# Re-ordering the borders of a four-layer graph network kernel: opening, layer changes, last round, and filler work for TensorE

## The chip, the cores and the metric

The kernel runs on one core of a Trainium2 chip. Time is device time in microseconds (us) of one execution. The kernel before takes 2108.0 us (median of 3 runs, 2107.67 to 2110.47). All runs of a timed comparison are compared with runs of the kernel before on the same chip. The changed kernel was not run again beside the experiments, which had other rounds on five chips; the kernel before had medians of 2107.0 to 2107.6 there, and 2108.59 beside the changed kernel. So a timed difference of some 1.5 us or less shows nothing by itself; there I go by the stages of the traces. A profiled execution also gives a trace, whose span is some 1.8 us shorter than its measured time (2103.9 for 2105.65).

## The reference

Four layers, each `x = x + layer(relu(layernorm(x)))`, on x of 128 samples x 64 nodes x 256 features, in float32:

```python
# layer 0: aggregate with the normalized adjacency, two products, two batch norms
A_norm = A + eye(n);  deg = A_norm.sum(0) + A_norm.sum(1) - diag(A_norm)
A_hat = A_norm * dinv[:, None] * dinv[None, :]           # dinv = rsqrt(deg)
agg = einsum('nm,bmd->bnd', A_hat, h)
out = batchnorm(relu(batchnorm(agg @ W1.T + b1)) @ W2.T + b2)
# layer 1: two graph convolutions, then LSTMs over windows of p = 1, 2, 3, 4 nodes
h = relu(einsum('ts,bsh->bth', adj, h @ Wg0 + bg0))
h = relu(einsum('ts,bsh->bth', adj, h @ Wg1 + bg1))
for p in 1..4: h[:, last node of each window] = lstm_last(h's windows of p nodes)
# layer 2: causal attention, one head;  layer 3: attention with 4 heads, masked by adj == 0
```

## The kernel before

The 8192 rows of x go in 16 chunks of 512. Layer 0 takes the first 268 us. Layer 1 goes by eight superchunks of two chunks, in which the LSTM's products fill TensorE and the convolutions of the next chunks are put in as units at chosen places (`CONV`). Layers 2 and 3 run interleaved, one `ROUND` a chunk, with a `FIRST` and a `LAST` round. Within these regions the program's order is the order of the instructions on each engine that is listed. So an instruction that waits can hold back those that stand behind it on its engine: a VectorE copy in the profile after (50.93) stands behind a step that waits 1.54 us.

```python
    with tc.manual_schedule(engines={PE, DVE, Pool, SP}):        # opening (engine names cut)
        xt = load0(0)                        # 512 KB of input
        ...                                  # adjacency, 4 small loads, then the weights
        an, dinv = degrees(setup)            # VectorE
        mv, rstd = ln_stats(xt, "a0")
        normalized(setup, an, dinv)          # scale, transpose on TensorE, scale
        ln_apply(hs[0], xt, mv, rstd, "a0")  # ScalarE
        norm0(1)
    ...
    CONV = (0, 2, 4, 5, 6, 7, 8), (7, 10, 11, 12, 13, 14, 15)
    ...
        for i in (0, 0, 1, 0, 1, 0, 1, 0, 1, 1, 0, 1, 0):    # border of layers 0 and 1
            next(convs[i])
    ...
    FIRST = """norm2+0 apply2+0 norm2+1 apply2+1 res1+14 ... chan2+0 q2+0 copyq2+0 v2+0 score2+0
               chan2+1 exp2+0 q2+1 ... v3+1"""
    LAST = """q2+0 exp3-2 sum3-2 apply3-1 divide3-2 copyq2+0 v2+0 score2+0 v3-2 ...
              turn3-1 score3+0 out3-1 store-1 v3+0 exp3+0 sum3+0 divide3+0 turn3+0 out3+0 store+0"""
```

`norm` takes statistics on VectorE (a power on GpSimd), `apply` scales on ScalarE, `chan` transposes on TensorE, `turn` transposes the softmax, `out` multiplies it by v, and `+0`, `-1` give the chunk relative to the round.

## Time and profile before

TensorE idles 62.8 us of a span of 2103.9. I call its work cold, or at half clock, where the same instructions take about twice the time that they take elsewhere (an aggregate 2.18 us instead of 1.16), and warm, or at full clock, elsewhere. The stages below run between anchors on TensorE's timeline that both kernels have.

| stage of the kernel before | from, to (us) | length |
|---|---|---|
| opening, to product 1 of the second chunk | 0, 33.04 | 33.04 |
| rest of layer 0, to the first transpose for layer 1 | 33.04, 268.84 | 235.80 |
| border, to the first LSTM product | 268.84, 304.53 | 35.69 |
| LSTM, to its last product's end | 304.53, 1672.31 | 1367.78 |
| first round, to chunk 3's q of layer 2 | 1672.31, 1747.06 | 74.75 |
| steady rounds, to the last chunk's q | 1747.06, 2040.70 | 293.64 |
| last round, to the end of the span | 2040.70, 2103.90 | 63.20 |

The lines of the profile from which the idle time and the half-clock stretches were read stand in the prediction.

### The profile page before, as it was taken

How to read it: one execution, taken by the hardware profiler on the slowest of the kernel's cores; microseconds unless marked ns; L12 is line 12 of the kernel's file. 1: busy time of each engine (PE TensorE's matmuls, PEld its weight loads, DVE VectorE, ACT ScalarE, POOL GpSimd, SP SyncE). 2: the span in 40 equal slices, each digit the busy share in tenths (PEclk: the TensorE clock that was granted, in tenths of full speed). 3: DMA queues.
4: the chain of work that ended last, by engine and by line, in shares of the span. 5: the costliest groups of instructions: out<-in, count | busy, mean ns of one | idle time of the engine just before them, and what ended most of it. 6: DMA issues, size and time to landing. Idle time of an engine off the chain costs nothing.

```text
span 2103.9 us, 29103 instructions
## 1 busy us (share of the span) xinstructions
PE 2041.1 (97%) x12181; PEld 1264.9 (60%) x12181; DVE 882.9 (42%) x1935; ACT 800.8 (38%) x1451; POOL 137.0 (7%) x192
## 2 busy tenths in 40 slices
PE   6999979999999999999999999999999989999997
PEld 3444444684575577468467557656736756676665
DVE  5644442333333333332432332433222256677774
ACT  5654323334334233333333423333333334444442
POOL 3100010000000000000000000000000011112211
PEclk9999989999999999999999999999999999999999
DMA  3202020101002002010100100200010100000000
GB/s 113 71 31 90 20 81 21 31 21 51 30 11 60 31 1 70 1 31 21 51 31 21 51 30 1 70 21 1 23 32 1 37 4 31 22 22 21 21 21 31
DMA packets 51860, 69.88 MB, mean 33 GB/s; under 512 B 4112, under 2 KB 45328, under 8 KB 51728
## 3 DMA queue, kind: packets, MB, share of 16 engines
q1 hardware_dynamic: 49312, 59.59, 9.1%
q0 software_dynamic: 2256, 8.40, 1.2%
q8 instruction: 96, 1.57, 0.3%
q14 instruction: 36, 0.29, 0.0%
q10 hardware_dynamic: 160, 0.03, 0.0%
HBM read 43.89 MB, written 24.12 MB: 32 GB/s over the span
## 4 chain that ended last, share of the span: by engine, by line
PE 82%; DVE 2%; ACT 1%; issue 0%; POOL 0%; DVEq 0%; ACTq 0%; POOLq 0%
PE g L522 37%; PE g L529 20%; PE p_q L640 5%; PE v L632 5%; PE v L479 3%; PE u L491 3%; PE p_k L640 3%; PE tc_n L186 1%; PE tr L667 1%; PE agg_b L175 1%; PE o L831 1%; PE agg_c L175 1%; PE s L732 1%; PE o L762 1%; PE s L791 1%; ACT gate L535 1%
## 5 line engine op out<-in xcount | busy, mean ns | idle before, releaser
L522 PE MATMUL g<-hT,wih 128*128 128x256 f32 (+2 forms) x2496 | 828.2, 484 | 9.7 <-ACT gate L545 7.1
L522 PEld LDWEIGHTS g<-hT,wih 128*128 128x128 f32 x2496 | 466.2, 188 | 336.1 <-issue 184.3
L535 ACT ACTIVATE gate<-g,bias 128x256 f32<-128x256 f32 (+2 forms) x624 | 349.6, 561 | 790.7 <-PE g L529 609.1
L529 PE MATMUL g<-hs,whh 128*128 128x256 f32 (+2 forms) x1536 | 435.8, 437 | 0.0
L529 PEld LDWEIGHTS g<-hs,whh 128*128 128x128 f32 x1536 | 291.3, 190 | 132.2 <-issue 62.0
L538 DVE TENSOR_TENSOR gate<-gate,gate 128x256 f32<-128x256 f32 (+2 forms) x96 | 47.7, 497 | 625.6 <-ACT gate L535 625.6
L545 ACT ACTIVATE gate<-cell 128x256 f32<-128x256 f32 (+2 forms) x176 | 90.0, 511 | 85.1 <-DVE cell L540 44.8
L544 DVE TENSOR_TENSOR cell<-gate,gate 128x512 f32<-128x512 f32 (+2 forms) x80 | 48.1, 602 | 169.5 <-ACT gate L535 169.2
L296 PE MATMUL z<-agg,w_sb 128*128 128x512 f32 x256 | 114.6, 601 | 0.0
L313 PE MATMUL z<-h,w_sb 128*128 128x512 f32 x256 | 110.2, 592 | 0.0
L156 ACT ACTIVATE h<-xs,nmr_n,rstd_n 128x256 f32<-128x256 f32 x128 | 66.3, 589 | 51.8 <-DVE nmr_n L154 51.8
L313 PEld LDWEIGHTS z<-h,w_sb 128*128 128x128 f32 x256 | 48.6, 190 | 60.7 <-issue 56.9
L296 PEld LDWEIGHTS z<-agg,w_sb 128*128 128x128 f32 x256 | 47.8, 191 | 55.6 <-issue 52.0
L548 DVE TENSOR_TENSOR hs<-gate,gate 128x256 f32<-128x256 f32 (+2 forms) x96 | 47.7, 497 | 74.1 <-ACT gate L545 47.0
L87 POOL TENSOR_SCALAR rstd_b<-mv_b 128x4 f32<-128x4 f32 x16 | 3.8, 240 | 1145.7 <-DVE mv_b L147 1072.4
L648 POOL TENSOR_TENSOR s<-s,mx 128x256 f32<-128x256 f32 (+1 forms) x32 | 40.2, 1257 | 471.3 <-PE tc_n L186 244.7
L635 ACT COPY v<-v 128x512 f32<-128x512 f32 x64 | 36.8, 580 | 80.9 <-PE v L632 80.9
L479 PE MATMUL v<-agg,wg_sb 128*128 128x512 f32 x128 | 60.8, 620 | 2.8 <-DVE agg L472 2.8
L640 PE MATMUL p_q<-hT,wqk_sb 128*128 128x512 f32 x128 | 59.9, 612 | 2.6 <-DVE hT L188 2.6
L640 PE MATMUL p_q<-hT,w_sb 128*128 128x512 f32 x128 | 61.8, 605 | 0.6 <-DVE hT L188 0.6
L640 PE MATMUL p_k<-hT,w_sb 128*128 128x512 f32 x128 | 60.1, 592 | 0.0
L632 PE MATMUL v<-w_sb,hT 128*128 128x256 f32 x256 | 59.5, 386 | 0.0
(144 smaller groups left out, 1901.1 us busy)
## 6 DMA issues: line engine op xcount, KB each, us to landing
xt<-in_x_dram SPq DMA_DIRECT2D x32, 512.0 KB, 4.1
far_h<-hm SPq DMA_DIRECT2D x16, 512.0 KB, 2.7
hT<-far_h SPq DMA_DIRECT2D x64, 128.0 KB, 3.5
out_dram<-o SPq DMA_DIRECT2D x16, 512.0 KB, 3.0
far_y<-ym SPq DMA_DIRECT2D x14, 512.0 KB, 2.7
y<-far_y SPq DMA_DIRECT2D x56, 128.0 KB, 3.0
wih<-in_wih_t_dram POOLq DMA_DIRECT2D x4, 1024.0 KB, 5.3
whh<-in_whh_t_dram POOLq DMA_DIRECT2D x3, 1024.0 KB, 5.2
```

The costliest lines, as they stand in the source:

```text
L156: nc.scalar.activation(dst[:, j, :], src[:, j, :], AF.Relu, bias=nmr[:, j : j + 1], scale=rstd[:, j : j + 1])
L296: nc.tensor.matmul(ps, w1_sb[:, k, m * P : (m + 1) * P], agg[:, k, :], start=(k == 0), stop=(k == KD - 1))
L313: nc.tensor.matmul(banks[c, m], w2_sb[:, k, m * P : (m + 1) * P], h1[c][:, k, :], start=(k == 0), stop=(k == KH - 1))
L479: nc.tensor.matmul(ps, wg0_sb[:, k, m * P : (m + 1) * P], agg[:, k, :], start=(k == 0), stop=(k == KD - 1))
L491: nc.tensor.matmul(ps[:, i, :], v[:, k, j * P : (j + 1) * P], wg1_sb[:, k, :], start=(k == 0), stop=(k == KD - 1))
L522: nc.tensor.matmul(banks[q][:, :n].rearrange("p (j w e) -> p j w e", w=nw, e=2), wi[:, k, o], hv[:, k, :, cols, :], start=(k == 0), stop=( ...
L529: nc.tensor.matmul(banks[q][:, :n], wh[:, k, o], hs[:, k, :n], start=False, stop=(k == KD - 1))
L535: nc.scalar.activation(g[q], banks[q][:, :n], AF.Tanh if q == 2 else AF.Sigmoid, bias=bs[:, q * KD + c : q * KD + c + 1])
L544: nc.vector.tensor_mul(cell[c], g[0], g[2])
L545: nc.scalar.activation(g[2], cell[c], AF.Tanh)
L632: nc.tensor.matmul(ps[:, i, :], hT[:, k, j * P : (j + 1) * P], w[:, k, first : first + D], start=(k == 0), stop=(k == KD - 1))
L640: nc.tensor.matmul(ps, w[:, k, m * P : (m + 1) * P], hT[:, k, :], start=(k == 0), stop=(k == KD - 1))
```

## The change

The intent is to close TensorE's gaps at the opening, at the borders and at the end, and to keep its clock up with transposes of the identity whose result nobody reads. The core of the diff, with cuts:

```diff
+    def keep_busy(n, name):
+        ps = bank(f"idle_{name}")
+        for i in range(n):
+            nc.tensor.transpose(ps[:, :P], ident, ident)
 ...                                     # product1(c)
+            if c == 0 and 2 * m == KH:
+                aggregate0(1)
+                ln_apply(hs[2], *stats2, "a2")
 ...                                     # opening
+        nc.sync.dma_start(xts[0][:, : NJ // 2], xr[0][:, : NJ // 2])
+        nc.scalar.dma_start(xts[0][:, NJ // 2 :], xr[0][:, NJ // 2 :])
         nc.gpsimd.dma_start(w1_sb, w1t.rearrange("(k p) f -> p k f", p=P))
+        nc.sync.dma_start(xts[1], xr[1])
 ...
         an, dinv = degrees(setup)
+        keep_busy(20, "a")
 ...
+        keep_busy(16, "b")
+        ln_apply(hs[0], xts[0], mv, rstd, "a0")
+        mv, rstd = ln_stats(xts[1], "a1")
+        aggregate0(0)
+        ln_apply(hs[1], xts[1], mv, rstd, "a1")
+        keep_busy(8, "c")
 ...                                     # layer 1
-    CONV = (0, 2, 4, 5, 6, 7, 8), (7, 10, 11, 12, 13, 14, 15)
+    CONV = (1, 1, 2, 3, 5, 7, 8), (7, 10, 10, 11, 12, 13, 14, 15)
+    FIRST = (0, 2, 2, 4, 5, 6, 7, 8)
+    EARLY = (1, 2, 7, 7), (8, 9, 13, 13)     # layer 2's norms of chunks 0 and 1
+    START = (0, 1, 0, 0, 1, 0, 1, 0, 1, 0, 1, 0, 1, 0, 1)
 ...
-        for i in (0, 0, 1, 0, 1, 0, 1, 0, 1, 1, 0, 1, 0):
+        for n, i in enumerate(START):
+            if n == 7:
+                keep_busy(30, "d")
+            if n == 8:
+                keep_busy(6, "e")
             next(convs[i])
 ...                                     # layers 2 and 3: the new FIRST and LAST
+    FIRST = """table+0 q2+0 norm2+2 copyq2+0 apply2+2 ...
+               out2+1 exp2+2 qk0+0 divide2+2 turn2+2 norm3+1 qk1+0 apply3+1 out2+2 score3+0 apply2+3
+               chan3+1 chan2+3 exp3+0 v3+0 sum3+0 divide3+0 norm3+2 qk0+1 turn3+0 qk1+1 out3+0 store+0
+               score3+1 v3+1"""
+    LAST = """... turn3-2 turn2+0 chan3-1 out2+0 out3-2 ...
+              score3-1 qk0+0 exp3-1 sum3-1 divide3-1 qk1+0 score3h+0 v3-1 exp3a+0 exp3b+0 sum3a+0
+              turn3-1 out3-1 divide3a+0 sum3b+0 divide3b+0 store-1 v3+0 turn3a+0 turn3b+0 out3a+0
+              storea+0 out3b+0 storeb+0"""
```

In `LAST`, steps with a and b do halves of the last chunk's softmax, transposes, product and output.

## The prediction

Where a cut is marked below, a passage stood. 10.0 + 10.3 + 0.3 + 12.9 + 9.0 = 42.5, less 1.5 for the clock, is 41, and 2108.0 less 41 is 2067. Two figures need a word. "1.95 us idle sufficed" means that the clock fell behind it: it is recorded as 1.00 from 1672 to 1674, 0.59 in the next 2 us and 0.50 from 1676 to 1679. And 0.122 us a transpose is an estimate of mine; in the trace of before mostly 8 take 1.04 to 1.09 us, 0.13 to 0.14 each.

> **What bounds the kernel now.** I read the page's busy shares first, then the slices, then TensorE's windows by stage, then TensorE's timeline in the stages that are not full.
>
> ```profile
> PE 2041.1 (97%) x12181; PEld 1264.9 (60%) x12181; DVE 882.9 (42%) x1935; ACT 800.8 (38%) x1451; POOL 137.0 (7%) x192
> PE   6999979999999999999999999999999989999997
> PEclk9999989999999999999999999999999999999999
> ```
>
> The kernel is bound by TensorE (PE): of the span of 2103.9 us it idles 62.8 us, and no other engine is above 42%. No product is removed by the change, so it can win only those 62.8 us and what half-clock stretches cost. The slices place both: the first, the sixth, one late and the last. The windows give sizes (third column: PE busy us, of the first column's):
>
> ```profile
> 0.00:40.00 40.00, 20.71 (x225) 11.46 (x225) 21.23 (x91) 17.45 (x31) 13.48 (x27) 1.00 0.42 135
> 240.00:320.00 80.00, 69.22 (x442) 38.95 (x441) 36.51 (x76) 21.66 (x38) 6.67 (x11) 0.91 0.24 79
> 1640.00:1680.00 40.00, 37.75 (x158) 29.76 (x157) 11.17 (x29) 15.95 (x34) 0.00 (x0) 0.93 0.08 32
> 1680.00:1760.00 80.00, 73.11 (x665) 49.61 (x664) 48.55 (x114) 31.71 (x58) 15.15 (x18) 0.97 0.07 18
> 2040.00:2104.00 64.00, 48.58 (x568) 32.67 (x558) 34.22 (x61) 17.69 (x31) 8.85 (x8) 0.95 0.08 26
> ```
>
> Idle: 19.3 (opening), 10.8 (layer 0 to 1), 2.3 + 6.9 (layer 1 to 2), 15.4 (end): 54.7 of the 62.8. The rest lies at LSTM borders: 7 of 0.62, and two gaps in the last superchunk (below). The timeline shows half clock as durations (start, duration; in brackets the idle before and who ended it):
>
> ```profile
> 17.11 2.18 PE L175 MATMUL agg_a<-ahat_t,h 64*64 64x64 f32 x64 [1.63 <-ACT h L156]
> 24.13 7.89 PE L296 MATMUL z<-agg,w_sb 128*128 128x512 f32 x16
> 275.14 2.12 PE L200 MATMUL at_b<-ident,y 128*128 128x128 f32 x8 [3.60 <-DVE y L445]
> 278.81 2.18 PE L175 MATMUL agg_b<-adjt_bd,h 64*64 64x64 f32 x64 [1.54 <-ACT h L156]
> 282.38 6.74 PE L479 MATMUL v<-agg,wg_sb 128*128 128x512 f32 x8 [1.40 <-DVE agg L472]
> 291.61 3.70 PE L479 MATMUL v<-agg,wg_sb 128*128 128x512 f32 x8 [1.40 <-DVE agg L472]
> 1576.97 12.51 PE L522 MATMUL g<-hT,wih 128*128 128x336 f32 x40 [1.81 <-ACT gate L545]
> 1623.57 6.62 PE L522 MATMUL g<-hT,wih 128*128 128x256 f32 x27 [1.51 <-ACT gate L545]
> 1674.25 2.81 PE L186 MATMUL tc_n<-ident,h 128*128 128x128 f32 x8 [1.95 <-ACT h L156]
> 1677.26 5.63 PE L640 MATMUL p_q<-hT,wqk_sb 128*128 128x512 f32 x8 [0.20 <-DVE hT L188]
> 1703.02 3.70 PE L640 MATMUL p_q<-hT,wqk_sb 128*128 128x512 f32 x8 [1.88 <-DVE hT L188]
> 1728.82 1.82 PE L667 MATMUL tr<-ident,s 128*128 128x128 f32 x8 [3.39 <-DVE s L658]
> 2094.28 1.94 PE L667 MATMUL tr<-ident,s 128*128 128x128 f32 x8 [4.52 <-DVE s L658]
> ```
>
> The same eight v products take 6.74 cold and 3.70 warm; warm aggregates take 1.16, cold 2.18. Summed in that way, cold stretches cost about 15 us: 3 opening, 5.3 layer 0 to 1, 6 layer 1 to 2, 1.5 end.
>
> [...]the eight v products above, at a recorded clock of 0.50. But 1.95 us idle sufficed at 1674, and with sparse work the half clock lasted from 275 to 288. [...]the change's filler is transposes. In the trace of before, only transposes ran from 1728.8 to 1732.2, and then the clock came back:
>
> ```profile
> 1731.00:1732.00 1.00, 1.00 (x7) 0.94 (x5) 0.84 (x2) 0.00 (x0) 0.00 (x0) 0.50 0.00 0
> 1732.00:1733.00 1.00, 1.00 (x47) 0.73 (x48) 0.22 (x1) 0.56 (x2) 0.00 (x0) 0.81 0.00 0
> ```
>
> I go with the trace: filler transposes warm the clock. [...]The trace has loads of 1.28 us with the next exp starting at once (1689.13, 1690.43): I count 1.28. [...]The trace: 512 KB of input landed 3.85 us after issue, while the small adjacency, queued with it, took over 5.
>
> **A, opening.** Before, VectorE starts the degrees at 10.81, after waiting for a bias of the LSTM (an add at 10.70), and does masks first. After, the adjacency goes first on the queues, the first input follows in halves on two queues, masks and biases move later; the first aggregate is followed by half of product 1 of chunk 0. Steps, by durations of before: adjacency there and degrees from 5.3; first chunk's statistics (2.1) 6.85 to 8.95; rows, transpose, scaling to 9.9 in gaps; norm applied (4 x 0.52) 10.3 to 12.6; aggregate of 64 to 12.9; z from 13.95, warm, because 44 filler transposes run in the gaps; the second aggregate comes between its halves. Sixteen z passes and an aggregate then put the second chunk's product at 23.05, against 33.04. **Gain 10.0.** Behind it TensorE is continuous, before and after.
>
> **B, layer 0 to 1.** From the idle at 268.84 to the first LSTM product at 304.53 before takes 35.7. The change turns both chunks at once, issues the LSTM weight loads later (GpSimd's power no longer stands behind an issue of 0.76), splits copies between VectorE and ScalarE, puts one u before the second v, and fills with 36 transposes. After: turns to 270.85; a dependence gap of norm (statistics 2.15, power 1.3) to 275.7; aggregate to 277.4, copy, v 278.35 to 281.8 (8 x 0.43), aggregate 282.9, u and v 3.45 each to 289.8, aggregate 290.9, u to 294.35. LSTM starts 294.35: **gain 10.3**, of which about 5.3 is clock.
>
> **C, superchunk borders.** Convolution units move by a place or two, so that an aggregate (1.09) covers the gap of about 0.5 to 0.6 between windows 1 and 2. But statistics on VectorE and a norm (4 x 0.52) on ScalarE now stand ahead of gates that TensorE waits for, 0.8 to 0.95 us. Six borders at -0.15 on balance. In the last superchunk a hoisted activation that preloads a table costs two loads of 1.28 in a loaded stretch. **Gain 0.3** (0 to 3.7 conceivable).
>
> **D, layer 1 to 2.** Norms of chunks 0 and 1 of layer 2 with their 16 transposes (1.0 per 8) move into the gaps of 1.81 and 1.51 in the last superchunk. So q starts straight behind the LSTM: no idle of 1.95, no cold start (2.81 + 5.63 for what warm is 1.0 + 3.44), and 2 us of transposes hidden. Before, the first round of layer 2 takes 1672.2 to 1747.06 = 74.9. After, its warm work is 56.9 (58.8 less the hidden transposes), and I find these stalls in the order on each engine: the transposes of chunk 2's softmax wait behind a copy of k (1.9), then 0.45 and 3.0 for the norm of chunk 3, which stands behind adds of chunk 2 on VectorE. 62.2, less overlap 0.2: 62.0. **Gain 12.9**, less 1 if the 3-us stall lets the clock fall.
>
> **E, end.** Score products and turns of the last chunk come earlier; its softmax, transposes and output go in halves. Before, the last round starts at 2040.70 and ends at 2103.9 = 63.2. After, by the same durations and the three stalls left (1.3 transposes, 1.7 for k behind a multiply, 1.8 attention copies), 54.2, including the last transfer's about 4.6. **Gain 9.0**, less 0.5 for clock.
>
> Filler: 80 x 0.122 = 9.8 us, all in idle time. **Sum**: 10.0 + 10.3 + 0.3 + 12.9 + 9.0 = 42.5, less 1.5 for clock: 41. From 2108.0: **2067**.
>
> **Rivals.** (1) The filler doesn't warm the clock[...]: A loses 3, B 5, so 2075. For it: [...]the long cold stretch with sparse work. Against: the rows at 1731. (2) New waits replace the old: [...]VectorE and ScalarE carry more at window borders and in the first rounds. For it: VectorE 48.6 of 80 busy at 1680 to 1760, the k copies, table loads. It takes back perhaps 8: 2075. (3) Transfers bound the opening: adjacency, 0.5 MB input and 1 MB of weights share the queues (337 GB/s at their best around 25). Weights would be there by about 8 by this estimate, so I doubt it; A would be 7: 2070. (4) Everything is hidden: the two borders of the last superchunk also close and no stall is left: 2055.
>
> **Range and chances.** Sizes of A, B, E are each sure to about 1.2, C to 2.5, D to 3; together about 5 by squares. Eighty in a hundred: 2060 to 2075. Two per cent lies at 2065.8, just beyond my middle: faster 0.43, within 0.56, slower 0.01.
>
> **What would show it.** A: the second product of chunk 1 near 23, aggregates of 1.1 to 1.2. B: LSTM at 284 on the new clock (294 less A's 10), v of 3.5. C: borders about as long as before. D: q directly behind the last LSTM product, ROUND 3's q some 62 later, stalls near 1.9 and 3. E: last round 54. The prediction is wrong if aggregates still take 2.18 behind filler, or if window borders grow by over half a us each.

## The result, and the profile after

The changed kernel takes 2071.85 us (median of 4, 2071.72 to 2072.81), the kernel before 2108.59 in the same rounds. The ratio is 0.9826, with a 95% interval of 0.9809 to 0.9843. Ratios are the mean time of one kernel's fast runs over that of the other's in the same rounds, so not quite the ratio of the medians. I had said 2067 in a range of 2060 to 2075; the gain is 36.7 us where I had 41. It stays short of two per cent (2065.8), the side to which I had given 0.56.

The changed kernel's page, its busy shares and slices:

```profile
PE 2039.9 (99%) x12261; PEld 1270.8 (61%) x12261; DVE 881.1 (43%) x1941; ACT 804.2 (39%) x1457; POOL 136.6 (7%) x192
PE   8999999999999999999999999999999999999998
PEclk9999999999999999999999999999999999999999
```

The 80 filler transposes are among the 12261 instructions. Of a span of 2070.1 us, 30.2 are idle now, 62.8 before, and no inner slice falls below nine tenths. By stages:

| stage | before | changed | gain | predicted gain |
|---|---|---|---|---|
| opening | 33.04 | 25.46 | 7.58 | 10.0 (A) |
| rest of layer 0 | 235.80 | 237.61 | -1.81 | 0 |
| border of layers 0 and 1 | 35.69 | 26.30 | 9.39 | 10.3 (B) |
| LSTM, with 16 transposes of layer 2 in it | 1367.78 | 1366.74 | 1.04 | 0.3 (C) |
| first round | 74.75 | 66.66 | 8.09 | 11.9 (D) |
| steady rounds | 293.64 | 293.65 | -0.01 | 0 |
| last round | 63.20 | 53.68 | 9.52 | 8.5 (E) |
| sum | 2103.90 | 2070.10 | 33.80 | 41 |

Two things are to be explained: which steps missed, and why the timed runs gain 2.9 us more than the two traces (36.7 against 33.8).

TensorE's timeline of the changed kernel, by the points of the prediction (start, duration; in brackets the idle before and who ended it):

```profile
2.67 4.43 PE L145 MATMUL idle_a<-ident 128*128 128x128 f32 x20 [2.67 <-POOL ident masks.py:199]
10.74 3.36 PE L145 MATMUL idle_b<-ident 128*128 128x128 f32 x16
14.03 1.16 PE L181 MATMUL agg_a<-ahat_t,h 64*64 64x64 f32 x64
25.46 7.13 PE L302 MATMUL z<-agg,w_sb 128*128 128x512 f32 x16
51.76 7.10 PE L302 MATMUL z<-agg,w_sb 128*128 128x512 f32 x16 [1.51 <-DVE agg L287]
272.94 3.67 PE L511 MATMUL v<-agg,wg_sb 128*128 128x512 f32 x8
485.91 1.17 PE L554 MATMUL g<-hT,wih 128*128 128x512 f32 x2 [0.38 <-DVE hT L585]
1655.94 3.60 PE L719 MATMUL p_q<-hT,wqk_sb 128*128 128x512 f32 x8
1690.35 0.44 PE L746 MATMUL tr<-ident,s 128*128 128x128 f32 x2 [1.79 <-DVE s L737]
1699.86 2.80 PE L192 MATMUL tc_n<-ident,h 128*128 128x128 f32 x8 [1.90 <-ACT h L162]
1702.45 5.73 PE L711 MATMUL v<-w_sb,hT 128*128 128x256 f32 x16
2052.04 0.70 PE L853 MATMUL s<-k,q 64*64 64x64 f32 x32 [1.59 <-DVE k L837]
2058.58 1.16 PE L897 MATMUL o<-v,att 64*64 64x64 f32 x64 [1.32 <-ACT att L751]
```

The first aggregate takes 1.16 us where it took 2.18, and v behind the border 3.67 where it took 6.74: full clock. Behind the LSTM the first q starts at once. But the 20 transposes of the first filler take 0.22 us each, half clock from first to last; 16 more, behind an idle of 3.37, take 3.36 us at half clock and end at 14.0, just when the aggregate starts; a product in layer 0, where TensorE used to be continuous (busy for all 235.80 us of the stage), waits 1.51; and in the first round an idle of 1.90 is followed by 8 transposes at 2.80 and v at 5.73, which are half-clock durations again.

The wait in layer 0, on VectorE's timeline of the changed kernel:

```profile
50.85 0.16 DVE L160 SCALAR_TENSOR_TENSOR nmr_a<-mv_a,rstd_a 128x4 f32<-128x4 f32 x1 [1.54 <-POOL rstd_a L88]
50.93 0.68 DVE L287 COPY agg<-agg_a 128x512 f32<-128x512 f32 x1
```

The copy of an aggregate that TensorE had done at 42.1 stands behind a norm step that waits 1.54 us for GpSimd's power. This stretch is ordered by the scheduler, which puts 23 instructions of VectorE between the end of that aggregate and the copy. In the kernel before, copies stood behind such waits, too:

```profile
44.99 0.16 DVE L154 SCALAR_TENSOR_TENSOR nmr_a<-mv_a,rstd_a 128x4 f32<-128x4 f32 x1 [1.54 <-POOL rstd_a L88]
45.07 0.68 DVE L284 COPY agg<-agg_a 128x512 f32<-128x512 f32 x1
```

That copy was done over 3 us ahead of its product (49.35) and did no harm.

### The profile page after: what moved, and what is told of

Same layout as the page of the kernel before. It is cut to its first block, busy times and chain, and to the rows that moved or that the text cites. A ratio compares the mean times of both kernels' runs of the same rounds, so it can differ in the third digit from the quotient of the medians.

```text
span 2070.1 us, 29270 instructions
## 1 busy us (share of the span) xinstructions
PE 2039.9 (99%) x12261; PEld 1270.8 (61%) x12261; DVE 881.1 (43%) x1941; ACT 804.2 (39%) x1457; POOL 136.6 (7%) x192
## 4 chain that ended last, share of the span: by engine, by line
PE 89%; DVE 4%; ACT 3%; DMA 2%; POOL 1%; issue 1%; SPq 0%; DVEq 0%; POOLq 0%; ACTq 0%
PE g L554 33%; PE g L561 20%; PE v L711 6%; PE p_q L719 5%; PE z L319 5%; PE z L302 4%; PE u L523 3%; PE v L511 3%; PE p_k L719 2%; PE tc_n L192 1%; ACT h L162 1%; ACT gate L567 1%; PE s L795 1%; PE agg_c L181 1%; PE tr L746 1%; PE o L897 1%
## 5 line engine op out<-in xcount | busy, mean ns | idle before, releaser
L727 POOL TENSOR_TENSOR s<-s,mx 128x256 f32<-128x256 f32 (+2 forms) x33 | 40.4, 1223 | 302.9 <-DVE mx L726 204.0
L523 PE MATMUL u<-wg_sb,v 128*128 128x256 f32 x256 | 58.1, 380 | 0.0
L711 PE MATMUL v<-wvo_sb,hT 128*128 128x256 f32 x256 | 57.9, 379 | 0.0
```

Source lines behind the costliest of these rows:

```text
L523: nc.tensor.matmul(ps[:, i, :], v[:, k, j * P : (j + 1) * P], wg1_sb[:, k, :], start=(k == 0), stop=(k == KD - 1))
L711: nc.tensor.matmul(ps[:, i, :], hT[:, k, j * P : (j + 1) * P], w[:, k, first : first + D], start=(k == 0), stop=(k == KD - 1))
```

## The experiments

Twelve kernels ran. All gave correct results. Unless said otherwise an edit is to the changed kernel (2071.85 us).

**1. Without filler.**

```diff
     def keep_busy(n, name):
-        ps = bank(f"idle_{name}")
-        for i in range(n):
-            nc.tensor.transpose(ps[:, :P], ident, ident)
+        return
```

> The changed kernel without its 80 filler transposes; nothing else differs. If the filler keeps or makes the TensorE clock full (my theory, from the clock rows of the kernel before): the first aggregate back at about 2.18 us instead of 1.16, products at the start of layer 0 partly at half clock, and the border of layers 0 and 1 (from the first transposes there to the first LSTM product, 26.3 us with filler) 29 to 32 us; in all slower by 5 to 8 us, 2077 to 2080. If transposes don't count for the clock[...]: within 1 us of 2071.9, or 1 us faster, because 16 transposes no longer stand ahead of the first aggregate (3.36 us at half clock, ending only at 14.0).

Measured: 2074.7 us (4 runs, 2073.9 to 2075.05), 2.85 slower: neither theory in size. The border's timeline in this run:

```profile
270.77 2.18 PE L179 MATMUL agg_b<-adjt_bd,h 64*64 64x64 f32 x64 [5.02 <-ACT h L160]
273.79 5.62 PE L509 MATMUL v<-agg,wg_sb 128*128 128x512 f32 x8 [0.84 <-ACT agg L501]
```

Behind an idle of 5.02 the aggregate and v run cold, at a recorded clock of 0.50 from 271 to 277; with the filler the clock is 1.00 from 270 to 277 behind an idle of 1.74. So the filler does hold the clock in this pair of runs. The border is 28.51 against 26.30 with it (2.2 us). In the opening, counted from the adjacency's transpose, the second chunk's product starts 16.2 us later without filler and 15.0 with it (1.2 us). But the border without filler is still 7.2 us shorter than before: the order does most of it, the filler a quarter.

**2. The norm of chunk 3 earlier in the first round.**

```diff
-  out2+1 exp2+2 qk0+0 divide2+2 turn2+2 ... out2+2 score3+0 apply2+3 chan3+1 chan2+3
+  out2+1 exp2+2 apply2+3 qk0+0 divide2+2 turn2+2 ... out2+2 score3+0 chan3+1 chan2+3
```

> The norm of chunk 3 for layer 2 is applied earlier in the first round of layers 2 and 3 (its small VectorE step before a copy of k, not behind the adds, mask steps and maximum of other chunks). Theory: the idle of 1.90 us at 1699.86 and the half clock that follows it go: 1.9 + 1.7 (8 transposes 2.80 to 1.09) + 2.1 (16 products 5.73 to 3.62) = 5.7 us faster, 2066. Rival: another wait takes its place or the clock falls anyway at another gap: 0 to 2 us faster.

Measured: 2065.49 us, 6.4 faster; the first round 60.81 against 66.66. The timeline of this run:

```profile
1696.59 1.64 PE L192 MATMUL tc_n<-ident,h 128*128 128x128 f32 x13 [0.16 <-ACT h L162]
1698.06 3.62 PE L711 MATMUL v<-w_sb,hT 128*128 128x256 f32 x16
```

The wait is gone, and v is back to 3.62. The theory held in mechanism and size.

**3. The same wait left, but filled.** A step of 14 filler transposes between `chan3+1` and `chan2+3`.

> The wait at 1699.86 is left, and 14 filler transposes (1.7 us at full clock) are put into it. If the idle of 1.9 us is what lets the clock fall: transposes behind it about 1.1 us and v about 3.6 as in steady rounds: 3.8 us faster, 2068. If the low density of work before it is the cause, or transposes don't count: no gain, up to 0.5 slower.

Measured: 2069.1 us, 2.75 faster; the first round 63.97. The timeline of this run:

```profile
1697.36 1.69 PE L145 MATMUL idle_f<-ident 128*128 128x128 f32 x14
1699.42 0.33 PE L192 MATMUL tc_n<-ident,h 128*128 128x128 f32 x1 [0.37 <-ACT h L162]
1701.50 3.62 PE L711 MATMUL v<-w_sb,hT 128*128 128x256 f32 x16
```

v is at full clock although its data come no earlier: the recorded clock is 1.00 from 1697 to 1708, where the changed kernel has 0.50 from 1700 to 1706. The idle, then, let the clock fall, and 14 transposes in 1.69 us were enough to hold it. The gain is 1 us under my number because the transposes behind the filler come one by one as ScalarE delivers the norm (waits of 0.37, 0.16, 0.16 and 0.17).

**4. The kernel before, profiled again.**

> The kernel before, unchanged, profiled a second time, because its profiled run took 2105.65 and its timed runs 2107.67 to 2110.47. Theory: the clock falls at other moments from run to run, so that one or two of its half-clock stretches (opening, 275 to 289, 1674 to 1683, 1728 to 1732) differ by 1 to 4 us from the first trace and all other stages are equal within 0.3. Rival: the difference is spread or lies in transfers of the opening.

Measured: span 2106.6 against 2103.9 in the first trace. Six stages agree within 0.21 us; the last round is 66.24 against 63.20. Its timeline in this second trace:

```profile
2049.88 1.98 PE L732 MATMUL s<-hT,q 128*64 128x64 f32 x30 [2.10 <-DVE q L718]
2076.87 3.68 PE L640 MATMUL p_q<-hT,w_sb 128*128 128x512 f32 x4 [0.35 <-DVE hT L188]
```

In the first trace the same instructions are warm behind the same waits:

```profile
2050.22 1.15 PE L732 MATMUL s<-hT,q 128*64 128x64 f32 x30 [2.11 <-DVE q L718]
2075.77 1.98 PE L640 MATMUL p_q<-hT,w_sb 128*128 128x512 f32 x4 [0.35 <-DVE hT L188]
```

The same program with the same gaps loses the clock in one run and not in the other: behind 2.10 us the recorded clock is 0.50 from 2050 to 2052 in the second trace, behind 2.11 it stays 1.00 in the first. The cost is of the size of the missing 2.9 us: the profiled run of the kernel before was a lucky one (2105.65), and its timed runs have a median 2.9 higher. Its other timed runs point the same way, without naming a stage: those of 2105.4 to 2105.9 had a mean granted clock of 0.993 or 0.994, those of 2109.4 and more 0.990.

**5. Weights of layer 0 later.** The 512 KB weight load moves from GpSimd's queue at 1.27 us to the queue of SyncE, behind the first half of the input.

> The changed kernel with its 512 KB weight load of layer 0 issued behind the adjacency and the first input, instead of at 1.27 us beside them. My prediction had the degrees start at 5.3; the trace has 6.57. If the weights' transfer delays the adjacency (theory): degrees start at 5.3 to 5.7, everything after the opening about 1 us earlier. Rival: four small transfers of 256-byte rows need that time by themselves: degrees at 6.1 to 6.9 as in the other runs, no gain.

Measured: 2069.63 us (2 runs), 2.2 faster. VectorE's first step of the degrees in this run:

```profile
3.93 0.29 DVE L107 TENSOR_TENSOR an<-adj_bd,ident 128x128 f32<-128x128 f32 x1 [2.77 <-DMA adj_bd<-in_adj_dram]
```

It starts at 3.93 instead of 6.57, more than expected, and at 3.71 to 3.93 in all three traces with this edit; in the others with the changed opening it starts at 5.73 to 6.67. (The edit moves the load in time and to another queue; which of the two counts was not separated.) The second step then waits for the transposed adjacency, so the norm is applied only 1.8 us earlier (10.16 for 11.93), and the half-clock filler and the aggregate behind it take another 0.7: 1.1 us arrive at the product (24.37 against 25.46). Even that is near the scatter: where the opening was left alone, the product starts at 24.73 to 26.48. The other 1.3 in the trace lie in the first round (65.32), whose half clock also shifts from run to run: 65.2 to 66.7 in the runs that left it alone.

**6. A longer first filler**: 52 transposes instead of 20.

> First filler of 52 transposes instead of 20, so that it lasts until the normalized adjacency's transpose. Theory: in the changed kernel TensorE idles 3.37 us behind the first filler, so the second filler runs at half clock (3.36 us for 16) and ends at 14.0, which holds the first aggregate back; with a clock kept full the 16 take 1.95 and the aggregate follows the norm's parts: it ends 0.6 to 0.8 us earlier (relative to the transpose of the adjacency: 4.0 instead of 4.7 us), and so does all that follows. Rival: the aggregate is bound by the norm on ScalarE alone: no gain; or the longer filler now stands ahead of the adjacency's transpose: 0.5 to 1 us slower.

Measured: 2071.11 us (2 runs), 0.7 faster. The timeline of this run:

```profile
11.12 1.91 PE L145 MATMUL idle_b<-ident 128*128 128x128 f32 x16
12.96 1.42 PE L181 MATMUL agg_a<-ahat_t,h 64*64 64x64 f32 x64
```

The theory and its second rival hold in part. The second filler is warm (1.91) and the aggregate ends 3.4 us behind the adjacency's transpose instead of 4.7; but that transpose itself stands behind the longer filler, 5.1 us behind the start of the degrees instead of 3.9. Counted from the degrees, product 1 starts 0.2 us earlier: nothing won. The 0.7 is within the noise. One thing was not separated: the longer filler closes the idle, and it is also longer at work. The first filler of 20 took the half-clock time throughout (4.43 us, 0.22 each). 52 took 8.50 us (experiment 6), 44 took 6.45 and 7.74 (experiments 11 and 12); by my estimate from these lengths the full-clock durations (some 0.12 us each) begin only after 3 to 6 us of filler.

**7. VectorE in the program's order in layer 0.**

```diff
-    with tc.manual_schedule(engines={mybir.EngineType.PE}):
+    with tc.manual_schedule(engines={mybir.EngineType.PE, mybir.EngineType.DVE}):
```

> In layer 0, VectorE's order is that of the program instead of the scheduler's, so the copy of an aggregate comes before the next chunk's norm step, which waits for GpSimd. Theory: the idle of 1.5 us at 50.2 in the changed kernel (product of chunk 4 waits for that copy) and 0.3 at 32.5 go: the stage from the second chunk's product to the border (237.6) becomes 235.8, 1.8 us faster, 2070. Rival: in program order VectorE stalls at each norm and new waits come up in layer 0: equal or up to 5 us slower.

Measured: 2088.58 us, 16.7 slower; the rest of layer 0 takes 253.38 instead of 237.61. The rival held, in a size that I had not seen. The wait of 1.51 is gone, but twelve aggregates take the time of this one,

```profile
41.37 1.94 PE L181 MATMUL agg_a<-ahat_t,h 64*64 64x64 f32 x64
```

instead of 1.16, with the clock at 9 tenths or more in every slice of the page, and a product waits 4.40 us for ScalarE at 161.44. It is one wrong place, not the scheduler's order as a whole, that costs 1.5 us.

**8. Convolution units moved back, wrongly.** `CONV = (2, 4, 4, 5, 6, 7, 8), (7, 10, 11, 11, 12, 13, 14, 15)`.

> The changed kernel with the convolutions of the following chunks at their old places within the LSTM (norm as one piece). The trace has 172.38 us from border to border with the change and 172.57 before. Theory: 6 borders at 0.19 us: 1.1 us slower, borders 172.57 again with a wait of 0.48 for a ScalarE gate. My prediction had minus 0.15 for each: then 0.9 us faster.

Measured: 2084.0 us, 12.2 slower, but this was not the old order: I had put the statistics with the norm, where before they stood with the additions. It shows what that place costs: the LSTM stage is 1377.46 against 1366.74. Statistics, GpSimd's power (1.54 us of waiting on VectorE) and the norm then come in one row ahead of the aggregate.

**9. Convolution units moved back, rightly.** `CONV = (2, 2, 4, 5, 6, 7, 8), (7, 10, 10, 11, 12, 13, 14, 15)`.

> A proper undoing of the superchunk part, which the run before this one was not: it had put the statistics behind the additions by two places, straight ahead of the norm, where in the kernel before they stood with the additions. Now: additions and statistics together, norm two places on, aggregate one further, as before. Theory: 172.57 us from border to border and a wait of 0.48 behind a ScalarE gate again, against 172.38 with the change: 6 borders at 0.19 plus the edges, 1 to 1.5 us slower than the changed kernel. Rival: something else in the changed kernel (GpSimd's order given by the program) also counts, then borders differ from 172.57 by over 0.3.

Measured: 2073.03 us, 1.2 slower, which is within the noise; but the LSTM stage takes 1367.93 against 1366.74, and 1366.65 to 1366.90 in the nine other traces with the new places. From border to border it takes 172.57 us again (484.84 to 657.41), and 172.38 with the change. The theory held.

**10. The old last round** in the changed kernel.

> The changed kernel with the last round of the kernel before; all else as changed. Two traces of the kernel before had that round at 63.20 and 66.24 us (the second with two more half-clock stretches), the changed kernel has 53.68. Theory: the part is worth 9.5 us where the clock stays up and some 12.5 where it falls, so timed runs 2081.4 to 2084.5, spread over more than 1.5 us, and the first six stages as in the changed kernel. Rival: the half-clock stretches of the last round come only with what precedes it in the kernel before: all runs within 0.5 us of 2081.4.

Measured: 2082.62 us, 10.8 slower; the last round 64.87, with one half-clock stretch more than the first trace of before (p_q 3.64 us, as in experiment 4). So the clock falls there behind the changed kernel, too. The spread is only 0.74 us: that part of my expectation missed.

**11. The waits taken away together**: experiment 5; a first filler of 44 and a second of 14; the copy of chunk 4's aggregate on ScalarE; in `FIRST` and `LAST` the places below.

```diff
-  FIRST: out2+1 exp2+2 qk0+0 divide2+2 turn2+2 ... score3+0 apply2+3 chan3+1
+         out2+1 exp2+2 divide2+2 apply2+3 qk0+0 turn2+2 ... score3+0 chan3+1
-  LAST:  turn3-2 turn2+0 chan3-1 ... exp3-1 sum3-1 divide3-1 qk1+0 score3h+0
-         ... turn3-1 out3-1 divide3a+0 sum3b+0 divide3b+0 store-1 v3+0 turn3a+0
+         turn3-2 chan3-1 turn2+0 ... exp3-1 sum3-1 qk1+0 divide3-1 score3h+0
+         ... turn3-1 v3+0 divide3a+0 sum3b+0 divide3b+0 out3-1 store-1 turn3a+0
```

> The changed kernel with the waits that the traces named taken away together: weights of layer 0 issued behind the first input (e5: degrees up to 2.6 us earlier) and the first filler of 44 transposes (e6), so the product of chunk 1 at about 23.2 instead of 25.46; the copy of chunk 4's aggregate on ScalarE, so 236.0 instead of 237.6 to the border; softmax division of chunk 2 and norm of chunk 3 ahead of a copy of k in the first round, 66.7 to about 59.5; in the last round a copy of k ahead of a division, chunk 15's transposes behind another chunk's, v ahead of the attention product: 53.7 to about 51. Sum 13 us: 2059. Rivals: each earlier start meets the next wait, half of it is left (2065); the scheduler's order in layer 0 gets worse (stage over 240).

Measured: 2057.47 us (2056.82 to 2058.01), 14.4 faster than the changed kernel. Stages: opening 22.87, rest of layer 0 236.06, border 27.43, LSTM 1366.70, first round 58.93, last round 50.56. All but the border came as expected; the border lost 1.1, with v at 4.13 us and so part of it at half clock. Experiments 6 and 8 show the same border at 27.65 and 27.45, though they don't touch it.

**12. Two more waits.** Border filler 43 instead of 30; in `FIRST` `qk0+1 qk1+1 turn3+0 score3+1 out3+0 store+0 v3+1`.

> The combined kernel with 43 instead of 30 filler transposes at the border of layers 0 and 1, which close the idle of 1.74 us that was left ahead of the first aggregate there, and in the first round of layers 2 and 3 the turn of chunk 0's scores behind both products of the next chunk (idle of 1.14 us). Theory: the border at full clock throughout, aggregate 1.16 instead of 2.18 and v 3.60 instead of 4.13, so 25.5 to 26.0 us in place of 27.43; first round 58.9 to about 57.8; 2055. Rival: the longer filler delays the aggregate by as much as it wins, and another wait takes the second: 2057.5.

Measured: 2055.42 us (2054.91 to 2055.65), ratio to the kernel before 0.9752 (0.9736 to 0.9769). The border is back at 26.32, the first round 57.60. That the longer filler did the former isn't shown: with 30 transposes the border took 26.30 to 26.32 in six traces and 27.43 to 27.65 in three (experiment 7 aside). Only the aggregate stayed at 1.93. I take it not to be cold but to follow the norm's parts as ScalarE delivers them: the 6 transposes behind it take 0.88 and v 3.67, and in the changed kernel, where it takes 1.94 at a recorded clock of 1.00, ScalarE takes 2.08 for the four parts. This version beats both kernels.

## Why the prediction was right or wrong

The middle was 4.9 us off, and the time lay within the range. The mechanisms were mostly right; sizes were off, one of them by a half-clock stretch. Some sums of the prediction don't come out as written: its cold stretches add up to 15.8, not about 15; B's figures give 10.2, not 10.3; the squares give 4.4, not 5. The LSTM began at 289.37, not at 284, since A and layer 0 had lost 4.2 and B 0.9.

**A, opening** (10.0 said, 7.6 came). The step that failed is "adjacency there and degrees from 5.3": they started at 6.57, and the norm 1.6 us late. I had set my rival 3 aside because the weights "would be there by about 8"; that was an estimate of their arrival and said nothing of what they delay meanwhile. Experiment 5 shows degrees at 3.93 when the load is issued later and on another queue. The second failed term is "aggregate of 64 to 12.9": I had the filler warm, but its first part never was, and the second lasted 3.36 us instead of 1.95 and held the aggregate up to 14.03. Experiment 6 shows it: with a warm second filler the aggregate ends 1.3 us sooner behind the adjacency's transpose. The sentence "Behind it TensorE is continuous, before and after" was wrong: 1.8 us were lost in layer 0, 1.5 of them to the copy behind a norm step; with that copy on ScalarE the stage was 236.06 (experiment 11).

**B, border** (10.3 said, 9.4 came). The sum was nearly right, and so was "of which about 5.3 is clock": the transposes, the first aggregate and the first v lost 5.1 us at half clock before, and nothing in the changed kernel (v 3.67; the aggregate's 1.94 us are at a recorded clock of 1.00). What failed is the filler's share of it, "A loses 3, B 5": without filler 7.2 us of the gain stayed, so the filler is worth 2.2 here and about 3 in all, not 8. The new order alone shortens the half-clock stretch (v 5.62 for 6.74, no cold transposes).

**C, superchunks** (0.3 said, 1.0 came). How 0.3 follows from six borders at -0.15 and two table loads the prediction doesn't say. The sign of "-0.15" a border was wrong: it was 0.19 faster each (experiment 9). I had the statistics and the norm delay gates that TensorE waits for. They do not: between two borders TensorE idles 0.59 us where it idled 0.62. Nor is the gap closed, though: the wait moved (0.38 and 0.20 behind the LSTM's own result, where 0.48 was behind a gate). Most of the 0.19 is busy time (171.79 for 171.95), which I can't explain. And the 16 transposes of layer 2 went into the LSTM for nothing, as said.

**D, layer 1 to 2** (11.9 said, 8.1 came): the largest miss. I had found the stalls in the order and named them: 1.9 for chunk 2's transposes (1.79 measured) and 3.0 for chunk 3's norm (1.90). What failed is the term "less 1 if the 3-us stall lets the clock fall": the clock fell behind 1.90 us of idle and cost 3.8 (transposes 2.80 for 1.09, v 5.73 for 3.62). A fourth stall I had not seen: 1.15 us ahead of the transposes of chunk 0's softmax in layer 3 (1712.76). Experiments 2 and 3 show both halves, the wait and the clock. I had read before that 1.95 us sufficed at 1674 and still counted a chance of it as 1.

**E, end** (8.5 said, 9.5 came). Stalls were 1.25, 1.59 and 1.32, for which I had 1.3, 1.7 and 1.8. But the timed gain is larger than the two traces say, and the old last round lost its clock in two of the three traces that have it: 10.8 by experiment 10, 12.6 by the second trace of before.

**Why the total came close.** Traces alone give 33.8, 7.2 below my 41. Some 2.9 came back, as far as one second trace tells, because I had computed from a trace of the kernel before that was faster than its median, and never asked why its profiled run was 2.4 us faster than the 2108.0 from which I subtracted. This part was luck.

**The rivals.** The first (filler doesn't count for the clock) fell. The second (new waits) held for the first round and for layer 0, and not for the superchunks. The third (transfers) was true of the degrees as far as experiment 5 shows it (3.93 for 6.57, with time and queue of the load changed together), and of part of A (1.1 us). The fourth, with all hidden, was set at 2055; it did not hold for the changed kernel, and experiment 12 reached 2055.4 only by further edits.

What stays open: which gaps let the clock fall in a given run could be told here only after it (2.10 us did in the second trace of before, and did nothing in experiment 10), and how the timed 2.2 us of experiment 5 divide between the opening (1.1 in the trace) and the shift of the first round.

## What to carry to other kernels

When a change closes gaps, list the gaps that it leaves, and count each of about 2 us twice: once for the wait, and once for the half-clock stretch that may follow it (here 1.90 us, and then 3.8). Filler work belongs where the engine idles anyway, but it goes into the same queue as the work that is waited for: check what it stands ahead of, at the slow clock (here 16 transposes took 3.36 us and held an aggregate up), and whether it is long enough to get beyond that clock at all (20 were not, 44 and 52 were). And compute a gain from the same kind of number on both sides: one profiled run can be lucky (2105.65 for a median of 2108.0), and a second trace of the kernel before costs little.

## What the traces show of clock, transfers and table load

- Transposes and the clock: behind 52 transposes of the identity in a row, the next 16 took 1.91 us (0.12 each), where behind an idle of 3.37 they took 3.36 (0.21 each), and 14 in a gap kept v at 3.62 us instead of 5.73.
- Idles and the clock: the clock fell behind single idles of 1.90 (changed kernel, 1699.86), 1.95 (kernel before, 1674.25) and 2.10 us (its second trace), not always: 2.11 did nothing in the first trace, and 2.10 nothing in experiment 10. At the border an idle of 1.74 left v at 3.67 in the changed kernel and was followed by 4.13 in experiment 11. In two traces p_q ran at half clock behind short waits in a row (3.68 us behind 0.47, 0.16 three times and 0.35 in the second trace of before, 3.64 behind 0.82, 0.16 three times and 0.35 in experiment 10); the first trace of before has the waits of the second and p_q at 1.98.
- Small loads beside a large one: the adjacency's loads of 16 KB, issued first, were used at 3.93 us when the 512 KB of weights were issued behind half of the input, and at 6.57 when they were issued at 1.27 on another queue.
- Table load: in the trace of the kernel before it takes 1.28 us at 1689.13, between a copy that ends at 1689.12 and the exp at 1690.43; nothing else lies between them on ScalarE.
- The recorded clock: it was 1.00 at 17 to 19 us in the kernel before while the aggregate took 2.18 us, the duration of half clock. In the changed kernel it was 1.00 during the first filler (0.22 us each) and 0.50 only from 10.5 to 13.5. In the opening, go by the durations.
